# A four-layer graph network: X centred early, the GRU output centred by the matrix that turns it back, the next norm in column groups, and 36 idle products on TensorE

## The chip, the core and the metric

The kernel runs on one core of one Trainium2 chip. The metric is the device time of one execution in microseconds, the median of the runs. A core has five engines with a queue each, which work in the order of their queues and wait for each other by semaphores: TensorE (PE in the profile; its weight loads are PEld), VectorE (DVE), ScalarE (ACT), GpSimd (POOL) and SyncE (SP), which here issues the transfers.

## The reference, cut to what matters

X has 3327 rows of 64 numbers, `adj` is 3327 x 3327. Four layers run one after the other, each as X = X + layer(norm(X)), where the norm takes off each row's mean, divides by the root of its variance and is followed by a ReLU: a hyperbolic layer, a decayed sum over the graph, a signed graph attention whose output goes through two GRU cells, and a second hyperbolic layer. The part that this change touches is the end of the third layer and the start and end of the fourth:

```python
def _layernorm(x, axis=-1, eps=1e-5):
    m = jnp.mean(x, axis=axis, keepdims=True)
    v = jnp.var(x, axis=axis, keepdims=True)
    return (x - m) / jnp.sqrt(v + eps)
...
    def gru_cell(x, h, w_ih, w_hh, b_ih, b_hh):
        ...
        n = jnp.tanh(inn + r * hn)
        return (1.0 - z) * n + z * h
```

The third layer adds to X the sum of the two GRU outputs, each row scaled by that row's diagonal element of `adj`. The fourth layer takes the norm of that X, needs the row's norm squared (`x2` in the kernel) and ends in X plus a combination of the normed row and a sum over the graph.

## The kernel before, in words

Rows are padded to 26 tiles of 128 (T = 26, P = 128, D = 64), so X lies in SBUF as 128 x 26 x 64. The tiles are worked on in two halves of 13 (`HALVES`), and in the third layer tile t of the first half and tile t of the second half are paired, 64 columns each, in turned arrays of 128 x 1664 (`oP`, `hP`, `deg`, `xh`), where a row is a feature and a column is a node. These arrays go through in four column groups (`COLS`: 4, 3, 3 and 3 tiles, 512 or 384 columns).

`hyperbolic_series` (L350) is called twice, for the first and for the fourth layer. In both calls it first prepares: mean, centring, squares, variance, root by bit trick with polish steps (`root_by_bits`), the norm `x2` of the positive part (L449 to L469), then factors, the normed rows `Xr` (L481), their 16-bit parts `hi` (L482, ScalarE) and `lo` (L484, VectorE), and their turning by TensorE (L542, L517) with copies out of PSUM by ScalarE and VectorE (L524, L522). POOL makes further columns (L436 to L506). Weights are multiplied in L560, summed in L562, and spread over the partitions in L576 and its copies. Then the loop over the 4 x 26 tiles of the adjacency runs (ScalarE's sigmoid L629, POOL's mask L632, TensorE's L643 and L644, ScalarE's arctangent L649, VectorE's L654, TensorE's sums L664 and L672). In the fourth layer the factors of each row follow (L736 to L860), and then the end: ScalarE scales `M` tile by tile (L923, 22 of them), VectorE scales and adds (L916, L919), and SP stores X in three pieces (L2104).

`plain_gat` (L1841) is the third layer: 26 blocks of masked sums (L1871) with small pieces of work hung on to them by a table (`todo`, block number to function), then `take`, `mean`, and eight steps of the GRU (two cells x four groups; `products` L1987 and L1992, `sigmoids`, `before_tanh`, `tanh`, `state`). `turn_back` (L2032) turns the sum of the GRU terms of a group back to node rows on TensorE, by products with the identity that accumulate up to four terms (L2043), or by a transpose for the last group (L2041); `scale` multiplies by the diagonal element (L2059 on ScalarE, 64 columns at a time; L2054 on VectorE for the last group); `use` adds to X (L2063). The eight PSUM banks are halves of four tiles: 0 and 1, 2 and 3, 4 and 5, 6 and 7. Group k is turned into bank 4 + k.

The order on ScalarE, VectorE, TensorE and POOL is that in which the program writes the instructions (`manual_schedule`); waits are put in by the tile framework from reads and writes, and a pool that takes over another pool's space waits tile by tile. The order at the end of the third layer is written out:

```python
                tanh(K - 1)
                scale(0)
                turn_back(1)
                scale(1)
                turn_back(2)
                state(K - 1)
                use(0)
                turn_back(3)
                use(1)
                scale(2)
                scale(3)
                use(2)
                use(3)
```

Of the kernel before, what the change touches and what calls it, by code (L numbers as in the profile page):

```python
# [49 lines left out]
def tile_gnn4(ctx: ExitStack, tc: tile.TileContext, x, adjT, att0, b0, w1, bias1, w_gat, a_gat,  # L50
# [296 lines left out]
            after.append(of_r)  # L347
        return wlr, bcol, cc, sqc, isqc, um2, maxn2

    def hyperbolic_series(r, params, ok, masks=None, done=None, ahead=None, then=None, checks=None):  # L350

# [10 lines left out]


        KE = D + 9
        left_row = rows[0 if r is None else 1]
        W = 512
        with ExitStack() as st:
# [60 lines left out]
            with room(name="hsp", bufs=1) as tp, room(name="hsps", bufs=2, space=PSUM) as ps, \  # L430
                    tc.manual_schedule(engines={mybir.EngineType.Activation, mybir.EngineType.DVE,
                                                mybir.EngineType.PE, mybir.EngineType.Pool}):
                H, R, sq, sr = [tp.tile([P, T, D], F32, name=n) for n in ("H", "R", "sq", "sr")]
                Xe = tp.tile([P, T, KE + 9], F16, name="Xe")
                E, Fe = Xe[:, :, D:KE], Xe[:, :, KE:]
                G.memset(X0, 0.0)  # L436
                G.memset(E[:, :, 6:], SX)
                for k, part in enumerate(f16_parts((1.0 - PB / PA) * SX)):
                    G.memset(Fe[:, :, 6 + k:7 + k], part)
# [4 lines left out]
                    return tp.tile([P, T], F32, name=name)  # L444


                mean, v, rv, ax, ia2 = [new(n) for n in ("mean", "v", "rv", "ax", "ia2")]
                for ts in HALVES:
                    V.reduce_sum(mean[:, ts], X[:, ts, :], axis=AX.X)  # L449
                V.tensor_scalar(mean, mean, 1.0 / D, None, op0=OP.mult)  # L450
                for ts in HALVES:
                    V.tensor_sub(H[:, ts, :], X[:, ts, :], wide(mean[:, ts]))
                    A.activation(sq[:, ts, :], H[:, ts, :], AF.Square)
                for ts in HALVES:
                    A.activation(R[:, ts, :], H[:, ts, :], AF.Relu)
                    A.activation(sr[:, ts, :], R[:, ts, :], AF.Square)
                for ts in HALVES:
                    V.reduce_sum(v[:, ts], sq[:, ts, :], axis=AX.X)
                V.tensor_scalar(v, v, 1.0 / D, LN_EPS, op0=OP.mult, op1=OP.add)
                sd, q1, q2 = new("sd"), new("q1"), new("q2")  # L460
                steps = root_by_bits(sd, q1, q2, v)
                next(steps)
                V.reciprocal(rv, v)
                for _ in range(3):
                    next(steps)
                V.reduce_sum(x2[:, HALVES[0]], sr[:, HALVES[0], :], axis=AX.X)
                for _ in steps:
                    pass
                V.reduce_sum(x2[:, HALVES[1]], sr[:, HALVES[1], :], axis=AX.X)  # L469
                if r is not None:  # L470
                    V.tensor_scalar(rv, rv, cc, None, op0=OP.mult)
                V.tensor_mul(x2, x2, rv)
                V.tensor_scalar(ax, x2, 1.0, None, op0=OP.subtract)
                V.reciprocal(ia, ax)
                V.tensor_scalar(root, x2, 1.0, None, op0=OP.max)
# [90 lines left out]
                    copy_on(on, XF[c][:, o, :], turned16(lambda t: Xp[:, t, D:], KE, *range(t, t + c[1])))  # L566
                V.tensor_mul(right, lr[:, :, 1], z)
                V.tensor_scalar(right, right, bcol, None, op0=OP.add)
                V.scalar_tensor_tensor(root, root, ROOT, zs, op0=OP.mult, op1=OP.mult)
                V.tensor_scalar(small["k"], ia, 0.5 * PF, None, op0=OP.mult)  # L570
                V.tensor_scalar(small["bx"], ax, -1.0, None, op0=OP.mult)
# [340 lines left out]
            with room(name="hse", bufs=1) as tp:  # L912
                ah, am = all_factors(tp)

                def scaled(a, f, ts):
                    V.tensor_mul(a[:, ts, :], a[:, ts, :], wide(f[:, ts]))  # L916

                def added(a, ts):
                    V.tensor_add(X[:, ts, :], X[:, ts, :], a[:, ts, :])  # L919

                own = slice(T - 4, T)
                for t in range(own.start):
                    A.activation(M[:, t, :], M[:, t, :], AF.Copy, scale=am[:, t:t + 1])  # L923
                for ts in HALVES:
                    scaled(Xr, ah, ts)
                    added(Xr, ts)
                scaled(M, am, own)
                for ts in HALVES[0], slice(T // 2, T - 6), slice(T - 6, T):
                    added(M, ts)
                    done(ts)  # L930
# [907 lines left out]

            then(H, hparts, banks, last_x, finish, close)

    def plain_gat(masks, zo, deg, first, wg, gru, H, parts, banks, last_x, finish, close):  # L1841

# [6 lines left out]
        with ExitStack() as st:  # L1851
# [47 lines left out]
            xh = [[pers.tile([P, HP], F32, name=f"xh{g}{o}") for o in range(2)] for g in range(2)]  # L1899
            oP = H.rearrange("p k o d -> p (k o d)")  # L1900
            wgT = pers.tile([D, D], F32, name="wgT")
            hundred = pers.tile([P, 1], F32, name="hundred")
            V.memset(hundred, -100.0)
            for _ in range(1):
# [35 lines left out]
                def inverse2():  # L1940
                    V.scalar_tensor_tensor(deg, deg, -1.0, r0, op0=OP.mult, op1=OP.mult)
                    V.scalar_tensor_tensor(deg, deg, 2.0, r0, op0=OP.add, op1=OP.mult)

                todo = {3: lambda: degrees(2, 4), 4: lambda: degrees(3, 6), 12: lambda: (weights2(4), inverse()),
                        13: lambda: turn(0, 6), 15: lambda: weights3(5), 17: inverse2, 19: lambda: turn(4, 7),
                        20: lambda: turn(8, 4), 23: lambda: turn(12, 6)}
                V.tensor_scalar(zo[:, 2 * T:2 * T + 2], zo[:, 2 * T:2 * T + 2], first, None, op0=OP.mult)
# [84 lines left out]
                def turn_back(k):  # L2032

                    terms = [oP] if k == C - 1 else [oP, hP, deg] if k > 1 else [oP, xh[0][0], hP, deg]
                    t0, n = COLS[k]
                    pt = turned[k] = bank(4 + k)
                    for t in range(n):
                        cs = slice((t0 + t) * P, (t0 + t + 1) * P)
                        for i, src in enumerate(terms):
                            if len(terms) == 1:  # L2040
                                PE.transpose(pt[:, t * P:(t + 1) * P], src[:, cs], ident)  # L2041
                            else:
                                PE.matmul(pt[:, t * P:(t + 1) * P], src[:, cs], ident, start=i == 0,  # L2043
                                          stop=i == len(terms) - 1)

                def of_bank(k):
                    n = COLS[k][1]
                    return turned[k][:, :n * P].rearrange("p (t h d) -> p h t d", h=2, d=D)

                def scale(k):  # L2050
                    t0, n = COLS[k]
                    o = scaled[k] = tp.tile([P, 2, 4, D], F32, name="x", bufs=2)
                    if k == C - 1:
                        V.tensor_mul(o[:, :, :n, :], of_bank(k),  # L2054
                                     d2[:, :, t0:t0 + n, None].to_broadcast([P, 2, n, D]))
                        return
                    for h in range(2):
                        for t in range(n):
                            A.activation(o[:, h, t, :], of_bank(k)[:, h, t, :], AF.Copy, scale=d2[:, h, t0 + t:t0 + t + 1])  # L2059

                def use(k):
                    t0, n = COLS[k]
                    V.tensor_add(X2[:, :, t0:t0 + n, :], X2[:, :, t0:t0 + n, :], scaled[k][:, :, :n, :])  # L2063

                for k in (2, 3):
                    mean(k)
# [18 lines left out]
                tanh(K - 1)  # L2085
                scale(0)
                turn_back(1)
                scale(1)
                turn_back(2)
                state(K - 1)  # L2090
                use(0)
                turn_back(3)
                use(1)
                scale(2)
                scale(3)
                use(2)
                use(3)

    def load():
        for ts in HALVES:  # L2100
# [10 lines left out]
    wt, bias, wg, gru = middle_weights()  # L2111
    zo = const.tile([P, 2 * T + 2 + EARLY + len(LATE)], F32, name="zo")
    first = const.tile([P, 1], F32, name="first")
    V.memset(first, 0.0)
    for o in (0, D):
        V.memset(first[o:o + 1, :], 1.0)
    with ExitStack() as ms:
        mid, rs = [ms.enter_context(ExitStack()) for _ in range(2)]
        masks = [None] * (T // 2)
        degs = []  # L2120

        def make_masks(ks):
            pool = ms.enter_context(room(name=f"masks{ks[0]}", bufs=1, side="right"))
            for k in ks:
                masks[k] = pool.tile([P, 2, NP], F8, name=f"mask{k}")

        def right():
            make_masks(range(T // 2 - EARLY // 2))
            pool = rs.enter_context(room(name="middle", bufs=1, side="right"))
            degs.append(pool.tile([P, NP // 2], F32, name="deg"))  # L2130
            return degs[0]

        make_masks(range(T // 2 - EARLY // 2, T // 2))
        pool = mid.enter_context(room(name="own", bufs=1))
        own = [pool.tile([P, 2, CW], F32, name=f"own{k}") for k in range(2)]
        hyperbolic_series(None, params, ok[:, 0:1], ahead=Ahead(masks, zo, own),
                          then=lambda e: plain_decay(
                              e, right, masks, zo, wt, bias, gru, of_r[0],
                              lambda *a: plain_gat(masks, zo, degs[0], first, wg, gru, *a)))
        rs.close()  # L2140
        mid.close()
        hyperbolic_series(r3, params3, ok[:, 2:3], masks, store, checks=Late(zo))
    V.reduce_sum(ok[:, 1:2], zo, axis=AX.X)


# [55 lines left out]
```

## Time and profile before

| what | value |
|---|---|
| median of 3 runs | 721.02 us (720.81 to 722.56) |
| the profiled execution's own time | 719.45 us |
| its span, first to last instruction | 717.7 us |
| mean granted TensorE clock | 0.972 of full |
| busy: TensorE, VectorE, ScalarE, POOL | 636.2, 532.8, 542.1, 433.4 us |

The stretches around the change, from the windows of the profile (busy us; clock as a share of full):

| stretch, us from the start | what runs | PE | DVE | ACT | POOL | clock |
|---|---|---|---|---|---|---|
| 382.9 to 426.9 | blocks of the attention | 43.98 | 14.55 | 19.38 | 0.00 | 0.96 |
| 426.9 to 447.4 | GRU steps | 20.14 | 17.83 | 18.77 | 0.79 | 1.00 |
| 447.4 to 461.3 | turning back, adding to X | 9.14 | 8.47 | 6.09 | 0.55 | 1.00 |
| 461.3 to 474.7 | norm of the fourth layer | 0.00 | 12.79 | 6.06 | 2.50 | 0.56 |
| 474.7 to 485.0 | turning and weights | 9.57 | 9.63 | 6.36 | 5.17 | 0.74 |
| 485.0 to 695.0 | loop over the adjacency | 208.06 | 153.90 | 180.90 | 172.81 | 1.00 |
| 695.0 to 705.3 | factors of each row | 0.16 | 9.25 | 1.10 | 0.00 | 0.67 |
| 705.3 to 717.7 | scaling, adding, storing | 0.00 | 6.07 | 5.36 | 0.00 | 0.50 |

Busy times of a stretch are sums over one engine's instructions; an engine whose busy time is near the stretch's length sets its pace, and where none is near it, they wait for each other. In a timeline row the first two numbers are start and duration, and a bracket gives the idle time ahead of the instruction and what ended it. Instructions of one engine overlap a little, so a duration is longer than the distance to the next one.

### The profile page before, as it was taken

Reading aid. Unit: us, or ns where it says so; the run is one execution under the profiler, and the core shown is the slowest. Engines: PE = TensorE matmul, PEld = TensorE weight load, DVE = VectorE, ACT = ScalarE, POOL = GpSimd, SP = SyncE. Lnnn points to the kernel's source line nnn. Section 1 sums busy time; section 2 is a strip of 40 time slices with the busy share of each in tenths; the row PEclk is TensorE's granted clock in tenths of the full one; section 3 lists DMA queues with packets and bytes.
Section 4 is the critical chain, followed back from the end, with each engine's and each line's share of the span. In section 5 each row is a group of like instructions: output and inputs, shape, how many; then the busy total and the mean of one; then the engine's idle time right before and its main releaser. Section 6 shows DMA issues by size and latency. Waiting matters only on the chain.

```text
span 717.7 us, 12120 instructions
## 1 busy us (share of the span) xinstructions
PE 636.2 (89%) x4291; PEld 261.4 (36%) x4291; DVE 532.8 (74%) x990; ACT 542.1 (76%) x718; POOL 433.4 (60%) x329
## 2 busy tenths in 40 slices
PE   0799999999999889989998999459999999999970
PEld 0522233333333333435445653443223433333320
DVE  5967778777777799999755428697776877778756
ACT  3688888888888695687881479359888888888853
POOL 2799999989999400205730000039888788887840
PEclk9999999999999999999999999969999999999995
DMA  3998888898878716489960000203325345443001
GB/s 64 313 301 274 259 268 266 277 288 273 268 245 271 258 69 215 137 291 333 402 243 1 2 1 1 95 18 96 89 82 147 105 120 146 116 119 115 25 1 52
DMA packets 61638, 119.25 MB, mean 166 GB/s; under 512 B 9568, under 2 KB 34048, under 8 KB 61568
## 3 DMA queue, kind: packets, MB, share of 16 engines
q1 hardware_dynamic: 57216, 118.38, 51.2%
q10 hardware_dynamic: 4352, 0.02, 0.3%
q8 instruction: 35, 0.57, 0.3%
q14 instruction: 35, 0.29, 0.1%
HBM read 115.64 MB, written 0.88 MB: 162 GB/s over the span
## 4 chain that ended last, share of the span: by engine, by line
PE 67%; DVE 12%; issue 6%; POOL 6%; ACT 4%; DMA 3%; ACTq 1%; POOLq 0%; DVEq 0%
PE slot L664 17%; PE slot L672 9%; PE slot L643 9%; PE slot L1564 9%; PE slot L644 8%; POOL sig L632 6%; PE slot L1578 5%; PE slot L1871 5%; DMA adj<-in 3%; PE slot L1987 2%; PE slot L2043 1%; PE slot L1992 1%; DVE X L1617 1%; ACTq L322 1%; ACT sig L629 1%
## 5 line engine op out<-in xcount | busy, mean ns | idle before, releaser
L654 DVE SCALAR_TENSOR_TENSOR sig<-slot,sig 128x768 f32<-128x768 f32 (+2 forms) x209 | 212.8, 1018 | 105.6 <-POOL sig L632 104.2
L649 ACT ACTIVATE slot<-slot 128x768 f32<-128x768 f32 (+1 forms) x208 | 177.2, 852 | 53.3 <-PE slot L644 53.1
L632 POOL TENSOR_TENSOR sig<-adj,sig 128x768 f32<-128x768 f32 (+2 forms) x105 | 201.7, 1943 | 12.9 <-ACT sig L629 8.4
L629 ACT ACTIVATE sig<-leftB,right 128x768 f32<-128x768 f32 (+2 forms) x210 | 203.5, 970 | 0.5 <-PE pt L517 0.5
L632 POOL TENSOR_TENSOR sig<-mask,sig 128x768 f32<-128x768 fp8e4 (+3 forms) x106 | 173.6, 1651 | 38.2 <-ACT sig L629 37.3
L664 PE MATMUL slot<-sig,Xr 128*64 128x384 f32 (+1 forms) x832 | 169.9, 526 | 3.7 <-DVE sig L654 3.4
L643 PE MATMUL slot<-XC,XT 128*128 128x384 f16 (+1 forms) x416 | 142.2, 342 | 3.1 <-ACT sum L682 1.7
L644 PE MATMUL slot<-XF,XE 73*128 73x384 f16 (+1 forms) x416 | 141.6, 340 | 0.0
L672 PE MATMUL slot<-sig,X 128*32 128x384 f32 (+1 forms) x832 | 94.2, 525 | 0.0
L1570 ACT ACTIVATE w<-slot,ebias 128x832 bf16<-128x832 f32 x76 | 69.0, 951 | 25.3 <-PE slot L1564 24.9
L664 PEld LDWEIGHTS slot<-sig,Xr 128*64 128x64 f32 x832 | 49.8, 135 | 85.7 <-issue 62.7
L643 PEld LDWEIGHTS <-XT 128*128 128x128 f16 x416 | 40.6, 98 | 93.8 <-issue 67.4
L1564 PE MATMUL slot<-mask,rest 128*128 128x416 fp8e4 x208 | 53.9, 341 | 5.0 <-ACT adj L1570 2.8
L1564 PE MATMUL slot<-mask,after 128*128 128x416 fp8e4 x208 | 53.4, 339 | 1.3 <-DVE deg L1588 1.3
L644 PEld LDWEIGHTS <-XE 73*128 73x128 f16 x416 | 40.8, 98 | 28.6 <-issue 4.0
L1459 DVE TENSOR_SCALAR_CACHE_REDUCE same<-late 128x832 fp8e4<-128x832 f32 x48 | 48.4, 1009 | 0.0
L219 POOL TENSOR_TENSOR mask<-mask,offdiag 128x128 fp8e4<-128x128 fp8e4 x26 | 17.5, 684 | 44.4 <-PE slot L1564 44.3
L436 POOL MEMSET X<- 128x832 f32 x2 | 1.6, 791 | 69.6 <-ACT xh L1978 69.6
L1871 PE MATMUL slot<-mask,own 128*64 128x384 fp8e4 (+1 forms) x416 | 39.6, 345 | 2.6 <-DVE deg L1588 2.6
L672 PEld LDWEIGHTS slot<-sig,X 128*32 128x32 f32 x832 | 16.4, 108 | 67.7 <-issue 67.7
L542 PE MATMUL pt<-ident_h,Xp 128*64 128x128 f16 x32 | 2.6, 314 | 37.7 <-ACT Xp L482 37.7
L1578 PE MATMUL slot<-w,h 128*64 128x416 bf16 x304 | 34.0, 345 | 0.0
(341 smaller groups left out, 696.2 us busy)
## 6 DMA issues: line engine op xcount, KB each, us to landing
adj<-in SPq DMA_DIRECT2D x78, 384.0 KB, 5.2
late<-in SPq DMA_DIRECT2D x48, 416.0 KB, 3.2
adj<-in SPq DMA_DIRECT2D x17, 832.0 KB, 7.2
adj<-in SPq DMA_DIRECT2D x27, 512.0 KB, 5.8
ahead<-in SPq DMA_DIRECT2D x14, 832.0 KB, 7.7
ahead<-in SPq DMA_DIRECT2D x16, 416.0 KB, 5.7
own<-in SPq DMA_DIRECT2D x16, 416.0 KB, 5.8
own<-in SPq DMA_DIRECT2D x8, 832.0 KB, 10.1
```

Source lines behind the costliest of these rows:

```text
L629: A.activation(sig[:, os], leftB[c][:, os], AF.Sigmoid, bias=right[:, b:b + 1])
L632: G.tensor_tensor(sig[:, os], adj[:, os], sig[:, os], op=OP.mult)
L643: PE.matmul(L[:, o, :c[1] * P], XT[:, rows], XC[c][:, o, :], start=True, stop=False)
L644: PE.matmul(L[:, o, :c[1] * P], XE[:KE, rows], XF[c][:, o, :], start=False, stop=True)
L649: A.activation(L, L, AF.Arctan, scale=PA / SX ** 2)
L654: V.scalar_tensor_tensor(sig[:, os], slot[:, os, :tiles[k][0][1] * P], PC, sig[:, os], op0=OP.add, op1=OP.mult)
L664: PE.matmul(acc[c][o * D:(o + 1) * D, 0, :n], Xr[:, b, :], sigs[k][:, o, :], start=b == 0, stop=b == T - 1)
L672: PE.matmul(acc[c][q:q + 32, 1, :n], X0[:, b - 1 + i, :], w[:, o, :], start=b == 1, stop=b == T - 1, tile_position=(0, q))
L1564: PE.matmul(cnt[o][:, h, :BK], w, cols(k, o, h), start=w is after and steps[k][1] == T - 1, stop=True, skip_group_check=True)
L1570: A.activation(ws[k][:, o, :, :], cnt[o][:, :, :BK], AF.Exp, scale=-LN2, bias=ebias)
L1578: PE.matmul(acc[c][o * D:(o + 1) * D, h, :BK], parts[i][:, b, :], w[:, o, h, :], start=b == T - 1 and i == 0, stop=b == 0 and i == 1)
L1871: PE.matmul(acc[k][o * D:(o + 1) * D, :], w, mask[:, of(k, o * HP)], start=n == 0 and i == 0, stop=n == T - 1 and i == 1)
```

## The change

The mean of X is taken off X early, in block 12 of the attention (`centre`), and kept in `ln.mean`. The GRU output is turned back by products with a matrix `centring` of 130 columns in place of the identity: the identity less 1/64 within each half of 64, which takes off the row mean, and two columns that give that mean. The means of the GRU output, scaled, go to `dm` and are added to `ln.mean`. The groups go to banks 4 and 5, 6, 0 and 2. The norm's squares, variance and `x2` are computed by column groups in tiles that the GRU no longer needs, and the fourth layer takes `H = X`, `rv` and `sd` from there. At the end the mean comes back as the bias of L923, and for the last four tiles by four activations in the preparation. 36 products of `ident_bf` with a slice of `diag` go into bank 7, which nobody reads. `X0` is zeroed by ScalarE in the fourth layer. The first layer's preparation is unchanged (`ln` is None there; it only moves into a branch).

```diff
+                if ln is None:
+                    G.memset(X0, 0.0)
+                else:
+                    A.activation(X0.rearrange("p t e -> p (t e)"), X[:, HALVES[0], :].rearrange("p t d -> p (t d)"),
+                                 AF.Copy, scale=0.0)
...
+                else:
+                    H, rv, sd = X, ln.rv, ln.sd
...
-                V.tensor_mul(x2, x2, rv)
+                V.tensor_mul(x2, x2s, rv)
...
+                if ln is not None:
+                    for t in range(own.start, own.stop):
+                        A.activation(X[:, t, :], X[:, t, :], AF.Identity, bias=ln.mean[:, t:t + 1])
...
-                    A.activation(M[:, t, :], M[:, t, :], AF.Copy, scale=am[:, t:t + 1])
+                    A.activation(M[:, t, :], M[:, t, :], AF.Identity, scale=am[:, t:t + 1], bias=ln.mean[:, t:t + 1])
...
+            BACK = P + 2
+            centring = pers.tile([P, BACK], F32, name="centring")
+            means = centring[:, P:]
+            G.memset(means, 0.0)
+            for o in range(2):
+                G.memset(means[o * D:(o + 1) * D, o:o + 1], 1.0 / D)
+            V.tensor_sub(centring[:, :P].rearrange("p (o d) -> p o d", o=2), ident.rearrange("p (o d) -> p o d", o=2),
+                         wide(means))
...
+                def centre():
+                    V.reduce_sum(ln.mean, X, axis=AX.X)
+                    V.tensor_scalar(ln.mean, ln.mean, 1.0 / D, None, op0=OP.mult)
+                    V.tensor_sub(X, X, wide(ln.mean))
-                todo = {3: lambda: degrees(2, 4), 4: lambda: degrees(3, 6), 12: lambda: (weights2(4), inverse()),
+                todo = {3: lambda: degrees(2, 4), 4: lambda: degrees(3, 6), 12: lambda: (weights2(4), inverse(), centre()),
...
-                    pt = turned[k] = bank(4 + k)
...
+                    for i in range(0, n, 3):
+                        m = min(3, n - i)
+                        pt = bank((4, 6, 0, 2)[k] + i // 3)[:, :m * BACK].rearrange("p (t x) -> p t x", x=BACK)
+                        for t in range(m):
+                            cs = slice((t0 + i + t) * P, (t0 + i + t + 1) * P)
+                            for s, src in enumerate(terms):
+                                PE.matmul(pt[:, t, :], src[:, cs], centring, start=s == 0, stop=s == len(terms) - 1)
+                        turned.setdefault(k, []).append(pt)
...
+                def new_means(k):
+                    t0 = COLS[k][0]
+                    for pt in turned[k]:
+                        ts = slice(t0, t0 + pt.shape[1])
+                        V.tensor_mul(dm[:, :, ts], pt[:, :, P:].rearrange("p t h -> p h t"), d2[:, :, ts])
+                        t0 = ts.stop
...
+                def use_at_once(k):
+                    t0, n = COLS[k]
+                    for h in range(2):
+                        for t in range(n):
+                            to = X2[:, h, t0 + t, :]
+                            V.scalar_tensor_tensor(to, of_bank(k, h, t), d2[:, h, t0 + t:t0 + t + 1], to,
+                                                   op0=OP.mult, op1=OP.add)
+                sq, pos, sr = xh[1][0], xh[1][1], xh[0][1]
...
                 tanh(K - 1)
                 scale(0)
                 turn_back(1)
-                scale(1)
                 turn_back(2)
                 state(K - 1)
+                turn_back(3)
                 use(0)
-                turn_back(3)
-                use(1)
+                squares(0)
+                positive(0)
+                use_at_once(1)
+                new_means(0)
+                new_means(1)
+                squares(1)
+                variance(0)
+                variance(1)
+                for _ in range(36):
+                    PE.matmul(bank(7), ident_bf, diag[:, :4 * P], start=True, stop=True)
                 scale(2)
                 scale(3)
+                use(3)
+                squares(3)
                 use(2)
-                use(3)
+                squares(2)
+                for k in (0, 1, 3, 2):
+                    if k:
+                        positive(k)
+                    squares_of_positive(k)
+                variance(3)
+                variance(2)
+                V.tensor_scalar(ln.v, ln.v, 1.0 / D, LN_EPS, op0=OP.mult, op1=OP.add)
+                steps = root_by_bits(ln.sd, *ln.qs, ln.v)
+                next(steps)
+                V.reciprocal(ln.rv, ln.v)
+                for between in (lambda: new_means(2), lambda: new_means(3),
+                                lambda: V.tensor_add(ln.mean, ln.mean, dm.rearrange("p h t -> p (h t)"))):
+                    next(steps)
+                    between()
+                norms2(0, COLS[2][0])
+                for _ in steps:
+                    pass
+                norms2(COLS[2][0], C2 - COLS[2][0])
```

`squares(k)` is ScalarE's square of the group's X into `sq`, `positive(k)` its ReLU into `pos`, `squares_of_positive(k)` the square of that into `sr`; `variance(k)` and `norms2` are VectorE's row sums of `sq` and `sr`.

## The prediction, made before the changed kernel was run

> **What bounds the kernel now.** I read the page first. Its slices show TensorE busy nearly everywhere, with one hole around slices 26 and 27, where the granted clock also falls:
>
> ```profile
> PE   0799999999999889989998999459999999999970
> PEclk9999999999999999999999999969999999999995
> ```
>
> One slice is 17.9 us, so the hole lies near 460 us, at the seam of the graph attention and the second hyperbolic layer. The timeline there (start, duration, engine, line, tiles, idle before and its releaser) says what the seam is made of:
>
> ```profile
> 450.88 0.39 PE L2043 MATMUL slot<-ident,deg 128*128 128x128 f32 x2
> 451.30 1.74 ACT L2059 ACTIVATE x<-slot,dcol 128x64 f32<-128x64 f32 x8 [0.41 <-PE slot L2043]
> 452.86 0.56 DVE L2027 TENSOR_TENSOR own<-hP,deg 128x384 f32<-128x384 f32 x1
> 453.10 0.49 PE L2043 MATMUL slot<-ident,own 128*128 128x128 f32 x2 [1.83 <-ACT x L2059]
> ...
> 457.89 0.49 PE L2041 MATMUL slot<-ident,own 128*128 128x128 f32 x3
> 458.42 1.33 ACT L2059 ACTIVATE x<-slot,dcol 128x64 f32<-128x64 f32 x6 [1.00 <-PE slot L2041]
> 459.78 0.56 DVE L2054 TENSOR_TENSOR x<-slot,dcol 128x384 f32<-128x384 f32 x1 [1.78 <-ACT x L2059]
> 460.26 1.02 DVE L2063 TENSOR_TENSOR X<-X,x 128x384 f32<-128x384 f32 x2
> 461.31 1.95 DVE L449 TENSOR_REDUCE mean<-X 128x13 f32<-128x832 f32 x2
> 463.50 1.96 DVE L452 TENSOR_TENSOR H<-X,mean 128x832 f32<-128x832 f32 x2
> 464.56 1.83 ACT L453 ACTIVATE sq<-H 128x832 f32<-128x832 f32 x2 [4.81 <-DVE H L452]
> 465.49 1.95 DVE L458 TENSOR_REDUCE v<-sq 128x13 f32<-128x832 f32 x2
> 467.48 0.18 DVE L459 TENSOR_SCALAR v<-v 128x26 f32<-128x26 f32 x1
> 470.17 1.01 DVE L469 TENSOR_REDUCE x<-sr 128x13 f32<-128x832 f32 x1
> 474.74 0.64 PE L542 MATMUL pt<-ident_h,Xp 128*64 128x128 f16 x8 [16.36 <-ACT Xp L482]
> 476.26 2.96 PE L517 MATMUL pt<-ident_h,Xp 128*128 128x128 f16 x26
> ```
>
> Two things are to be seen. The second turning back waits for ScalarE's scaling of the first (1.83 us), because banks 4 and 5 are halves of one PSUM tile. Then everything runs in series on whole halves of X: add, mean, subtract, square, reduce, root. TensorE stands idle 16.4 us. The windows around the hole give the clock (columns: busy us of the five engines, clock, DMA share, GB/s); the last row is the same preparation in the first layer:
>
> ```profile
> 462.00:463.00 1.00, 0.00 (x0) 0.00 (x0) 1.00 (x2) 0.00 (x0) 0.00 (x0) 0.98 1.04 389
> 463.00:464.00 1.00, 0.00 (x0) 0.00 (x0) 0.93 (x3) 0.00 (x0) 0.00 (x0) 0.50 0.77 310
> 480.00:481.00 1.00, 0.84 (x12) 0.66 (x12) 0.91 (x4) 0.47 (x1) 0.00 (x0) 0.99 0.41 83
> 22.00:23.00 1.00, 1.00 (x16) 0.83 (x11) 1.00 (x3) 0.20 (x2) 0.92 (x2) 1.00 0.87 234
> ```
>
> Last, the end, which the change also touches:
>
> ```profile
> 705.36 5.36 ACT L923 ACTIVATE M<-M,am 128x64 f32<-128x64 f32 x22 [5.20 <-DVE am L860]
> 709.34 2.03 DVE L919 TENSOR_TENSOR X<-X,M 128x832 f32<-128x832 f32 x3
> ```
>
> ScalarE ends at 710.72; VectorE's third addition begins at 710.81. They are level: any time added to L923 is added to the end.
>
> **Part 1, work moved early, at nothing.** The mean of X (reduce, scale, subtract over 1664 columns: 1.95 + 0.18 + 1.96 = 4.1 us by L449, L450, L452) goes to block 12, behind L1934, which ends at 401.0. VectorE then waits 9.74 us for ScalarE before L1941. The cover holds; without it the 4.1 us would delay L1941, whose result is first needed at 427. The matrix costs three small memsets on a POOL that is idle from 380 to 438, and one 128x128 subtraction (0.2 us) while TensorE streams blocks until 426.9.
>
> **Part 2, turning back.** Each 128-column fp32 product now takes 130 columns: 0.224 us apart today, so 0.227. The last group becomes products instead of transposes (0.11 to 0.23 each). The turns go to banks 4/5, 6, 0, 2, so the wait of 1.83 us is gone. From 447.4: 40 products, 40 x 0.227 = 9.1, tail 0.2: TensorE ends at 456.7 (now 458.4). The groups end at 451.3, 454.0, 456.1, 456.7. Group 2 also needs state(6), done at 451.3, and group 3 state(7), done at 453.4: neither is late.
>
> **Part 3, norm by groups.** VectorE's queue is now the limit. From rows: addition of 384 columns 0.56 (0.47 apart), of 512 0.69 (0.60 apart), 64-column fused add 0.197 apart (four L1617 took 0.87), independent small op 0.10, dependent 0.21. ScalarE: 384 columns 0.51, 512 0.61.
> - state(7) ends and scale(0) is in at 453.4; use(0) to 454.0; six fused adds of group 1 (1.2) to 455.2; three small products of means to 455.5.
> - squares(0) and (1) lie on ScalarE meanwhile (done 454.8, 455.8); variance(0), (1) on VectorE to 456.6.
> - scale(3) at 456.8, use(3) done 457.9; scale(2), six at 0.2, from 456.1 to 457.45; use(2) done 458.4.
> - squares(3), (2) done 458.5 and 459.0; variance(3), (2) done 459.55.
> - The scalar steps from there: now L459 at 467.48 leads to L469's end at 471.18, 3.7 us. The new list has three more small operations (0.3) and norms over 896 and 768 columns instead of 832 and 832: 3.85. Its inputs, squares of the positive part, end on ScalarE at 460.4 (groups 0, 1) and 462.2 (all): in time. So 459.6 + 3.85 = 463.4.
>
> The mean, the subtraction and L453 to L456 have left the seam. 471.18 - 463.4 = 7.8 us gained.
>
> X0's zeroing moves from POOL to ScalarE (0.9 us), ahead of L482's two copies. By the order of the pools X0 lies over the tile of squares, so it waits for the last norm: 463.4 to 464.4. L482 is not ready before 463.4 + 2.6. Hidden; 0.9 us at most if not.
>
> **Part 4, 36 products.** L643 shows one 512-column 16-bit product each 0.2175 us: 7.8 us. They queue behind the last turn and the reads of bank 6 (same tile): 456.7 to 464.5. What stands behind them is L542, ready at 463.4 + 3.56 = 467.0. No delay, 2.5 us spare. After the last product of today the clock stayed up 4.6 us (458.4 to 463), so 2.5 us of idling should keep it up. At half rate they would take 15.6 us, to 472.3, and hold L542 by 5.3 us.
>
> What is a warm clock worth? The Trainium skill (TensorE: Matmul & The Clock Gate, "What's actually happening") has the clock halved when idle and restored after some 3.4 us of work: by it the 5.3 us from 474.74 to 480 would run in half, and 2.6 us be won. The row says otherwise: in those 5.3 us VectorE goes without a gap from the second L484 through copies and root steps to L562 at 480.27, 0.15 us after it could. TensorE finishing sooner wins that 0.15. Also, L517 takes 2.96 us in the first layer too, under a recorded 1.00: the record doesn't show a cold start. I take 0.15; bounds 0 and 1.
>
> **Part 5, the mean put back.** Four one-bias activations (about 1.05 us) go before ScalarE's leftB copy, which waits 1.83 us for TensorE: hidden. The 22 of L923 get a second per-partition operand. Here a rule speaks against the change: the skill (ScalarE: Activation LUTs, "What ACT_TABLE_LOAD costs") adds about 93 ns for each pointer operand. No row here has two. With one, 64 columns take 0.333 (0.239 apart); without, L1928's 128 columns take 0.270, so 64 about 0.22: the first pointer costs about 0.1. Read as one fetch the second is free; by the rule 22 are 0.332 apart and end at 712.76, not 710.72. VectorE's third addition then begins 1.97 us later, and SP's last store and the branch behind it with it. I take the rule, since the first pointer obeys it; bounds 0 and +2.0.
>
> **Sum.** -7.8 - 0.15 + 1.97 = -6.0. The profiled execution took 719.45 us (span 717.7); I expect a span near 711.8. The median 721.02 stands 0.2% above that execution; the same difference gives 715.1.
>
> **Rivals.**
> - The second pointer is free: -7.95, 713.1. For it: both are [128,1] reads ahead of the same stream. Against: the first is paid for.
> - The seam shrinks less. Every group crosses engines (product, scale, add, square, reduce), and six of these hand-overs could cost 0.3 to 0.6 us more each than my 0.04: 2 to 4 us lost, 717 to 719. For it: DVE waits "issue" of 0.2 to 0.8 us at 708 and 709. Against: the present seam's hand-overs are short.
> - The idle clock is paid for: warm TensorE brings 1 us or more, 714 or below. Against: VectorE's full queue.
> - Slower: the filler products delay the layer. If their release comes only with the last read of a turned bank (the means of group 3, about 460.5), TensorE has idled 3.8 us; at half rate (0.435 each, 15.7 us) they end at 476.2, L542 starts 1.4 us later than today, and with the end's 2.0 us the time is 724.4. From a filler end past 472.9 the change loses. Against: group 3 lies in another tile, so they start warm, straight behind 40 products.
> - The change doesn't do what it says: X's norm moved but the last turn still sets VectorE's pace. It does already in my list, through use(3) and use(2).
>
> **How the numbers follow.** Likeliest, rule and list hold: 0.58, 714.1 to 716.1. Free pointer or paid clock: 0.19, 712.5 to 714. Seam shrinks less: 0.17, of it a third within 0.3% (about 2.2 us, what a measurement here can tell from no change). Slower by filler: 0.04, and 0.02 for anything else. Range 712.6 to 717.9. Faster 0.88, same 0.07, slower 0.05.
>
> **What would show it.** Right: L542 near 467 with idle before it under 3 us; clock 1.00 through 455 to 485; last norm's reduce ending near 463.4; L923's line at 0.33 us apart. Wrong: idle of VectorE at scale(3) or use(2) over 0.5 us; L542 released by the products; a second-layer loop that isn't just shifted.

## The result, and the profile after

The changed kernel takes 714.17 us (median of 4 runs, 713.11 to 714.82) beside 721.37 us for the kernel before in the same runs: ratio 0.9897, 95% interval 0.9879 to 0.9915. The forecast was 715.1. The profiled execution took 714.07 us, span 712.3.

First the page of the kernel after, the same slices as before:

```profile
PE   0799999999999889989998999989999999999960
PEclk9999999999999999999999999999999999999985
```

The hole is gone and so is the 6 in the clock. Then the timeline of the seam:

```profile
456.65 7.93 PE L2172 MATMUL slot<-diag,ident_bf 128*128 128x512 bf16 x35
...
456.85 0.56 DVE L2091 TENSOR_TENSOR x<-slot,dcol 128x384 f32<-128x384 f32 x1 [0.18 <-PE slot L2069]
457.44 1.03 DVE L2101 TENSOR_TENSOR X<-X,x 128x384 f32<-128x384 f32 x2
...
462.64 0.95 DVE L2133 TENSOR_REDUCE wt<-xh 128x12 f32<-128x768 f32 x1
...
467.01 0.41 PE L553 MATMUL pt<-ident_h,Xp 128*64 128x128 f16 x8 [2.43 <-ACT Xp L493]
```

VectorE's wait at scale(3) is 0.18 us, the last norm ends at 463.59, the filler at 464.58 and the layer's first turning product starts at 467.01. But a little later ScalarE meets a wait that the kernel before did not have, ahead of the loop's first sigmoid:

```profile
474.99 0.60 ACT L535 ACTIVATE leftB<-pe 128x512 f32<-128x512 f32 x1 [0.98 <-PE pe L590]
...
477.05 2.38 ACT L643 ACTIVATE sig<-leftB,right 128x512 f32<-128x512 f32 x3 [1.46 <-DVE XE L533]
```

In the kernel before, the sigmoid follows the copy without a wait:

```profile
482.95 0.60 ACT L524 ACTIVATE leftB<-pe 128x512 f32<-128x512 f32 x1 [1.83 <-PE pe L576]
483.45 1.32 ACT L629 ACTIVATE sig<-leftB,right 128x512 f32<-128x512 f32 x2
```

And the end:

```profile
698.80 7.40 ACT L936 ACTIVATE M<-M,mean,am 128x64 f32<-128x64 f32 x22 [5.19 <-DVE am L874]
...
705.57 1.22 DVE L933 TENSOR_TENSOR X<-X,M 128x448 f32<-128x448 f32 x2 [1.29 <-ACT M L936]
```

Single executions differ by up to 3.0 us in when the turning back begins (446.8 to 449.8 us), in a part to which this change adds only what runs hidden in block 12 and before it, and the median of the kernel before moves from 720.4 to 721.4 between the sets of runs below. So I compare traces from that point on: every time in the next table, and below where it says "after the turning back" or gives such a time alone, counts from the first product of `turn_back(0)`. These times repeat to 0.02 us where nothing differs.

| us after the turning back begins | before | after | difference |
|---|---|---|---|
| last norm's reduce ends (L469, L2133) | 23.76 | 15.98 | -7.78 |
| first turning product (L542, L553) | 27.32 | 19.40 | -7.92 |
| sum of weights lr (L562, L573) | 32.85 | 24.71 | -8.14 |
| first sigmoid (L629, L643) | 36.03 | 29.44 | -6.59 |
| scaling of M (L923, L936) begins | 257.94 | 251.19 | -6.75 |
| last addition ends (L919, L933) | 263.95 | 259.18 | -4.77 |
| last instruction | 270.29 | 264.74 | -5.55 |

Up to lr the forecast holds within 0.2 us. Then 1.55 us are lost ahead of the first sigmoid (from lr to it, 4.73 instead of 3.18), 1.98 at the scaling, and 0.8 come back behind the last addition.

### The profile page after: what moved, and what is told of

It is laid out like the page before. It is cut to its first block, busy times and chain, and to the rows that moved or that the text cites. A ratio compares the mean times of both kernels' runs of the same rounds, so it can differ in the third digit from the quotient of the medians.

```text
span 712.3 us, 12219 instructions
## 1 busy us (share of the span) xinstructions
PE 643.0 (90%) x4329; PEld 264.7 (37%) x4330; DVE 534.5 (75%) x1002; ACT 545.5 (77%) x723; POOL 432.1 (61%) x331
## 5 line engine op out<-in xcount | busy, mean ns | idle before, releaser
L643 ACT ACTIVATE sig<-leftB,right 128x768 f32<-128x768 f32 (+2 forms) x210 | 203.5, 970 | 1.7 <-DVE XE L533 1.5
L1622 POOL TENSOR_TENSOR X<-X,bias 128x256 f32<-128x256 f32 (+1 forms) x7 | 5.3, 786 | 44.4 <-DVE Xr L1637 44.4
```

The source lines that it names most:

```text
L643: A.activation(sig[:, os], leftB[c][:, os], AF.Sigmoid, bias=right[:, b:b + 1])
```

## The experiments

**The filler.** Without it, and with twice as much:

```diff
-                for _ in range(36):
-                    PE.matmul(bank(7), ident_bf, diag[:, :4 * P], start=True, stop=True)
```

> The changed kernel without the 36 filler products. Theory (VectorE's full queue sets the pace of the preparation, the clock does not): the same time as the changed kernel, 714.2 within 0.7 us; the turned XC products stand 0.64 us instead of 0.41 us, the layer's first sigmoid moves by 0.3 us at most. Rival (a warm TensorE is worth its halved work): 1 to 2.6 us slower, 715.2 to 716.8.

Median 715.71 us (ratio 0.9935, interval 0.9912 to 0.9958), more than the 0.7 us away that I allowed. lr came at 24.85 instead of 24.71, about the 0.15 of the prediction. The first sigmoid, though, came at 30.58 instead of 29.44, 1.14 us later where I allowed 0.3. The clock was still down when the weights were spread over the partitions (L590). TensorE without filler, then with 36:

```profile
474.89 2.02 PE L590 MATMUL junk<-ident,left 128*128 128x128 f32 x8
```

```profile
472.90 1.16 PE L590 MATMUL junk<-ident,left 128*128 128x128 f32 x8 [0.25 <-DVE left L574]
```

My theory had no place for that. The end came at 265.89 instead of 264.74, a loss of the rival's size; the medians' intervals overlap a little, so this is the word of one trace each.

```diff
-                for _ in range(36):
+                for _ in range(72):
```

> The changed kernel with 72 filler products instead of 36. They should end near 456.7 + 72 x 0.2175 = 472.3 us and hold the preparation's first turning product, now at 467.0, by 5.3 us. Theory (the products stand in TensorE's queue ahead of the layer): 4.5 to 5.5 us slower, near 719.3; a clock held at full speed through the preparation gives back no more than 0.3 us of it. Rival (they can be passed or hidden, or the warm clock pays): under 3 us slower.

720.07 us (0.999, 0.9966 to 1.0014); the filler ends at 24.74 and the first turning product moves from 19.40 to 24.67: 5.27 us, all of it on the path up to there. From that product to lr only 4.07 us passed instead of 5.31, so 1.2 us were given back where I allowed 0.3. The clock held, and VectorE could work ahead meanwhile; the pair of kernels with the banks alone, below, puts the clock's part at 0.14, and that VectorE's lead gave the rest is argued, not shown. The last instruction came 4.2 us later than with 36, a little less than the 4.5 expected.

```diff
-                for _ in range(36):
+                for _ in range(46):
```

> The changed kernel with 46 filler products, which end 19.15 us after the turning back begins; the layer's first turning product comes at 19.40. Theory (36 are too few: the clock falls for one or two windows of 3.4 us right when the preparation begins, and where it is still down the spreading of the weights takes 2.0 us instead of 1.2): no fall of the clock from the blocks to the end of the loop, the first turning product unmoved at 19.4, the sum lr within 0.2 us of the 24.7 of before, the first sigmoid no later than 29.4, and 0 to 1.2 us won against single executions with 36. Rival (VectorE's queue alone sets the pace): nothing moves by over 0.2 us.

715.13 us (0.9899, 0.9876 to 0.9922). The filler ends at 19.13, the first turning product stays at 19.41, lr at 24.71. But the clock did not hold. Two windows of this kernel (columns as in the prediction):

```profile
472.00:473.00 1.00, 0.84 (x22) 0.68 (x19) 0.93 (x4) 0.43 (x2) 0.52 (x4) 1.00 0.26 61
...
474.00:475.00 1.00, 1.00 (x6) 1.00 (x6) 0.67 (x6) 0.20 (x1) 0.00 (x0) 0.50 0.47 112
```

In them TensorE is at work, and the clock falls between them, 25.1 us after the turning back begins, on the spreading of the weights itself, and the first sigmoid came at 30.64, later than with 36. The expectation was wrong in this execution; in two others with 46 products at the same times (all repairs together, below) the clock held.

All falls between the blocks and the loop last 3.41, 6.83, 13.65 or 17.07 us, multiples of 3.413, and where such a window begins differs between executions. With 36 the clock fell 20.7 us after the turning back for one window in the traces of the changed kernel and of the next experiment, and at 21.3 and 21.7 us for two windows in those of the second pointer. What decides it is not shown. That the preparation's products are too small to keep the clock up is one reading. The idle pieces between them are another: TensorE was busy 2.44 and 2.40 of 3.41 us in the two windows ahead of the fall, and in the two traces where the clock held with 46 it was busy at least 2.59 in each window from the filler's end through the spreading.

**The wait for Xe.** By the order of the pools, the loop's first sigmoid tiles lay over H, R, `sq` and `sr` before, which had long been read; these tiles are no longer made, and Xe has moved into their place, which TensorE reads last.

```diff
+                else:
+                    gap = tp.tile([P, 4, T, D], F32, name="gap")
+                    V.memset(gap[:1, 0, 0, :1], 0.0)
```

> The changed kernel with an unused tile of 26.6 KB a partition ahead of Xe in the fourth layer's preparation, so that Xe lies where it lay before the change and the loop's first sigmoid tiles do not lie over it. Theory (the first sigmoid waits 1.5 us for the last transposes of Xe, because its tile takes over Xe's space): that wait is gone, the first sigmoid starts right behind the copy of leftB, and the kernel is 1.0 to 1.6 us faster, 712.6 to 713.2. Rival (the time between preparation and end is lost elsewhere in the loop): no change, 714.2.

The median, 715.45 us (0.993, 0.9902 to 0.9957), lies above the 712.6 to 713.2 expected and doesn't tell this kernel from the changed one. The trace does: the sigmoid follows the copy at once,

```profile
475.97 0.60 ACT L538 ACTIVATE leftB<-pe 128x512 f32<-128x512 f32 x1 [0.99 <-PE pe L593]
476.46 1.32 ACT L646 ACTIVATE sig<-leftB,right 128x512 f32<-128x512 f32 x2
```

at 27.88 instead of 29.44, and the last instruction comes at 263.42 instead of 264.74. The place of a tile was the whole loss ahead of the sigmoid: from lr to it 3.16 us, where 3.18 passed before the change.

**The second pointer.**

```diff
-                    A.activation(M[:, t, :], M[:, t, :], AF.Identity, scale=am[:, t:t + 1], bias=ln.mean[:, t:t + 1])
+                    A.activation(M[:, t, :], M[:, t, :], AF.Copy, scale=am[:, t:t + 1])
```

> The changed kernel whose last scaling of M (22 activations) takes the scale alone, as before the change; the mean of X is left out of the output of 22 tiles. Theory (each second pointer costs 93 ns and the last addition waits for it): the 22 take 5.36 us instead of 7.40, the last addition ends 2.0 us earlier, the kernel is 1.2 to 2.0 us faster, 712.2 to 713.0. Rival (the end is set by SP's stores and branch, whatever ScalarE does): under 0.6 us faster.

713.87 us (0.9909, 0.988 to 0.9938), above the 712.2 to 713.0 expected.

```profile
700.32 5.36 ACT L936 ACTIVATE M<-M,am 128x64 f32<-128x64 f32 x22 [5.20 <-DVE am L874]
...
704.31 2.03 DVE L933 TENSOR_TENSOR X<-X,M 128x832 f32<-128x832 f32 x3
```

From the scaling's start to the last addition's end 6.02 us instead of 7.99, the 1.97 of the prediction. From there to the last instruction 6.07 instead of 5.55, so 1.46 us remain. In this execution the clock was down for two windows at the spreading, and the first sigmoid came at 30.62; that hides the gain in the totals (264.48 against 264.74).

```diff
+            mean_back(range(14))
             region.close()
...
+                mean_back(range(14, own.start))
                 for t in range(own.start):
+                    A.activation(M[:, t, :], M[:, t, :], AF.Copy, scale=am[:, t:t + 1])
```

> The changed kernel, but the mean is put back on X itself by 22 activations with a bias alone, 14 of them after the loop's last copy and 8 after the tanh, where ScalarE idles; L936 takes the scale alone again. Theory (the second pointer is paid on the path, ScalarE's idle stretches of 3.8 and 5.2 us are free): the scaling takes 5.36 us again, the last addition ends 2.0 us earlier against the loop's end, the span 1.2 to 1.5 us earlier. Rival (the new activations delay the tanh or the additions): less than 0.5 us won, or slower.

714.33 us (0.9895, 0.9873 to 0.9917). The 14 stand behind the loop; the other 8 came to stand in ScalarE's idle pieces of the preparation, not behind the tanh. Neither group delays anything: from the first sigmoid to the scaling 221.79 us (221.75 in the changed kernel), from the scaling to the last instruction 12.04 instead of 13.54. So 1.5 us won, with all of X computed; the first sigmoid was at 30.42, again with two low windows.

**The early mean.**

```diff
-                ... 12: lambda: (weights2(4), inverse(), centre()),
+                ... 12: lambda: (weights2(4), inverse()),
...
                 turn_back(3)
+                centre()
```

> The changed kernel with X's mean taken off behind the last state instead of in block 12 (same three VectorE operations, 4.1 us, now in the seam). Theory (VectorE's queue is the limit of the seam and block 12 hid them): the last norm ends 4.0 us later against the turning back, 20.0 instead of 16.0, and the kernel is 3.5 to 4.1 us slower, near 718. Rival (ScalarE or TensorE sets the seam's pace): under 2 us.

719.57 us (0.9967, 0.9949 to 0.9985). The last norm ends at 19.80 instead of 15.98, 3.82 us later:

```profile
467.98 0.94 DVE L2133 TENSOR_REDUCE wt<-xh 128x12 f32<-128x768 f32 x1
```

VectorE's queue is the limit of the seam, and block 12 hides the three operations. The kernel loses more than the 3.5 to 4.1 us expected: its last instruction comes at 270.07, 5.3 us later. Of the rest, 1.25 us lie between lr and the first sigmoid, where the clock was down from 25.7 to 32.5 us.

**The banks alone, in the kernel before.**

```diff
-                    pt = turned[k] = bank(4 + k)
+                    pt = turned[k] = bank((4, 6, 0, 2)[k])
```

> The kernel before, with only the banks of the turning back changed: groups go to banks 4, 6, 0 and 2 instead of 4, 5, 6 and 7; still transposes with the identity and the old order. Theory (the second turn waits 1.83 us for ScalarE because banks 4 and 5 are one tile): that wait is gone, the last turn ends 1.8 us earlier, but the rest of the seam stays in series on whole halves, so the last norm ends 0.9 to 1.8 us earlier (22.0 to 22.9 us after the turning back instead of 23.8): only a small part of the 7.8 us. Rival (the banks carry the gain): 3 us or more.

718.65 us (0.997, 0.9947 to 0.9992). The last norm ends at 20.88 instead of 23.76: 2.88 us, more than I allowed, and just under the rival's 3. The rows of this kernel behind the third group:

```profile
456.14 1.34 ACT L2059 ACTIVATE x<-slot,dcol 128x64 f32<-128x64 f32 x6 [0.67 <-PE slot L2043]
...
456.46 0.56 DVE L2054 TENSOR_TENSOR x<-slot,dcol 128x384 f32<-128x384 f32 x1 [0.41 <-PE slot L2041]
457.51 1.03 DVE L2063 TENSOR_TENSOR X<-X,x 128x384 f32<-128x384 f32 x2 [0.49 <-ACT x L2059]
```

Three waits are gone, not one. The second turn's 1.83 us for ScalarE is one. ScalarE's scaling of the third group now begins 0.04 us behind that group's own products; before, it began 0.36 us behind them, because it waited for the last group's transposes in the other half of the same tile (most of its 1.00 us of idling was for its own products). And VectorE's scaling of the last group (L2054) no longer stands behind ScalarE's of the third, so the addition follows ScalarE at once and not 0.5 us later.

With the mean late, 3.96 of the 7.78 us at the last norm are left, and the banks alone bring 2.88. About 1.1 us remain for the column groups, the additions of group 1 in one operation each and the matrix. That is a difference of single traces, and no run has these alone.

```diff
+                for _ in range(72):
+                    PE.matmul(bank(5), ident_bf, diag[:, :4 * P], start=True, stop=True)
```

> The kernel with only the banks changed, and 72 filler products behind the last turn, which end near 25.0 us after the turning back begins, before the layer's first turning product (near 26). Theory (a held clock helps the spreading of the weights only where it would have been down there; in the kernel before it was just back up by then): against the kernel with the banks alone the sum lr comes 0 to 0.3 us earlier and the first sigmoid 0 to 1.2 us earlier. Rival (a warm TensorE halves the preparation's TensorE time): 2 us or more.

717.87 us (0.9953, 0.9933 to 0.9973). The clock held from the filler into the loop. TensorE's 26 transposes then wait for VectorE between groups (TensorE's timeline):

```profile
473.56 0.84 PE L517 MATMUL pt<-ident_h,Xp 128*128 128x128 f16 x12
474.60 0.61 PE L517 MATMUL pt<-ident_h,Xp 128*128 128x128 f16 x8 [0.20 <-DVE XC L522]
475.47 0.49 PE L517 MATMUL pt<-ident_h,Xp 128*128 128x128 f16 x6 [0.26 <-DVE XT L522]
```

lr at 29.82 against 29.96 with the banks alone, first sigmoid 32.98 against 33.14: the 0.15 of the prediction. In the banks' kernel the spreading was warm without filler too.

**All repairs together.** Unused tile, 46 fillers, mean in ScalarE's idle time:

> The changed kernel with all three repairs: the unused tile ahead of Xe, 46 filler products, and the mean put back in ScalarE's idle time. Theory (three separate losses of 1.2 to 1.5, 0 to 1.2 and 1.2 to 1.5 us): from the turning back to the end 261.9 us against 264.7, or 711.4 us where the changed kernel takes 714.2; ratio to the kernel before 0.984 to 0.987. Rival (they share one wait): under 2 us won.

711.71 us (0.985, 0.9823 to 0.9876), against 714.17 us and 0.9897 for the changed kernel; the intervals just part. First sigmoid 27.88, last addition 255.84, last instruction 261.91 us after the turning back, as expected. And once more, beside the same kernel without any filler:

> The kernel with the unused tile ahead of Xe and the mean put back in ScalarE's idle time, and no filler products at all. Theory (without filler the clock is down from before the preparation and comes back with a window that begins anywhere; if it is still down at the spreading of the weights, those 16 product passes take 2.0 us instead of 1.2 and the first sigmoid waits for them): lr 0.14 us later than with filler, and the first sigmoid at 28.0 us after the turning back where the clock is up in time, at 29.0 to 29.4 where it is not; 0.1 to 1.5 us slower than with 46. Rival (VectorE's queue hides it all): 0.2 us at most in every execution.

> The kernel with all three repairs once more, on the same chip as the one without filler. Theory: first sigmoid at 27.9 us after the turning back where the clock holds and up to 29.4 where a window of low clock falls on the spreading of the weights; end at 261.9 to 263.4; ratio to the kernel before 0.983 to 0.988, and 0.1 to 1.5 us faster than without filler. Rival: the two are the same.

Without filler 712.17 us (0.9877, 0.985 to 0.9904), with it 712.49 us (0.9892, 0.9852 to 0.9932): the medians can't tell them apart. The traces can. TensorE without filler, then with it:

```profile
472.81 2.02 PE L593 MATMUL junk<-ident,left 128*128 128x128 f32 x8
474.62 1.50 PE L593 MATMUL pe<-ident,left 128*128 128x128 f32 x8
```

```profile
475.08 1.16 PE L593 MATMUL junk<-ident,left 128*128 128x128 f32 x8 [0.82 <-DVE left L577]
476.08 1.06 PE L593 MATMUL pe<-ident,left 128*128 128x128 f32 x8
```

lr differs by 0.14 us, the first sigmoid by 1.49 (29.36 against 27.87), the last instruction by 1.43 (263.28 against 261.85). That is one execution of each. The mean granted clock is on record for every execution: with all repairs it is 0.984 or more in seven of eleven, as in both traces where the clock held, and 0.979 to 0.981 in four. One low window is worth 0.0024 of it (3.41 us at half, in some 710), so one or two more were low in those four, though not necessarily on the spreading. How often that happens, with or without filler, and whether the filler pays, stays open.

## Why the prediction was right, and where its sum was off

- **Part 1** held. `centre` ran from 401.3 to 405.3 us, with VectorE still idle 5.6 us behind it; out of its cover it costs 3.82.
- **Part 2**: the times held (groups end within 0.2 us of the list), but "the wait of 1.83 us is gone" was two thirds of what the banks bring (2.88). The other two waits stood in the prediction's own fence, in the brackets of the rows at 458.42 and 459.78. A product of 130 columns stands 0.223 us from the next, as one of 128 did, and not 0.227. The sum did not suffer, because the list was built forward and not as a difference.
- **Part 3** held: the last norm at 15.98, forecast 16.0 (463.4 - 447.4). VectorE's queue was read rightly as the limit; the rival that every hand-over costs 0.3 to 0.6 us more fell.
- **Part 4** failed in three places. "2.5 us of idling should keep it up": in none of the five traces with 36 did it. "The record doesn't show a cold start" was a misreading of the row at 22 us: the clock's records in that trace begin only at 26.05 us, and the 1.00 ahead of them stands for no record. The products there were as slow as under 0.50 (row below the list). And "I take 0.15" is right for the copies (0.14 and 0.14 in two pairs) but left out the spreading of the weights, where nothing of VectorE's hides TensorE. In the kernel before the clock was back at 480.03 us, 0.8 us before that work, and I took this for its nature; it was luck. Where it is down, the first sigmoid comes about 1.0 to 1.5 us later. The estimate from the Trainium skill's rule of an idle window (TensorE: Matmul & The Clock Gate, "What's actually happening") was 2.6 us won; 1.49 is the most that a pair of traces shows. In the changed kernel's trace the clock was low for the transposes and up for the spreading, so this error did not show in its time.
- **Part 5** held to the hundredth for the last addition: 0.332 us apart, 1.97 us. That the end moves with it was wrong by about a quarter (1.46 us in the second pointer's experiment): with the additions further apart the tail behind the last one shrank from 6.34 to 5.55. Of these 0.79 us, 0.45 lie at SP's last store and its read of the flag behind it (0.86 us before, 0.50 after), and 0.3 in the program's last wait, which I have not explained.
- **The step that was missing**: that the loop is "just shifted". I placed X0 against the tiles of the norm, but not what comes to lie in the room of the four tiles that the change does away with. That cost 1.55 us ahead of the first sigmoid, and 1.3 at the end.

The row of the first layer that part 4 misread; the same products took 0.64 us at 474.74 under 0.50, and 0.41 at 467.01 in the changed kernel under 1.00:

```profile
20.75 0.64 PE L542 MATMUL pt<-ident_h,Xp 128*64 128x128 f16 x8 [20.75 <-ACT Xp L482]
```

The sum, measured from the turning back: -8.1 at lr, +1.55 at the sigmoid, -0.2 in the loop, +2.0 at the scaling, -0.8 in the tail: -5.6, where -6.0 was forecast. That it came so near is luck in part: the 1.55 us at the sigmoid were not forecast, nor were the 0.8 in the tail and 0.2 each at lr and in the loop that made up for most of them. The medians' difference is 7.2 us, with an interval of 6.1 to 8.7 by the ratio. That is more than the traces' 5.6. Only one execution of each kernel has a trace, and the one of the kernel before was 1.9 us faster than its median here; where the rest lies is not shown.

## What to carry to other kernels

Write out the queue of the engine that limits a seam, operation by operation with the durations of rows; it gave the end of this one to 0.02 us, and its steps to 0.2. Then ask of every tile that a change removes what will lie in its place, and who reads that last. If an operand costs time on instructions that the end waits for, move its work to a stretch where that engine idles.

## What the runs showed of the hardware that was not expected

The clock changes in windows of 3.413 us: every low stretch between the blocks and the loop is one, two, four or five of them long. In one of three traces with 46 fillers it fell 5.7 us after TensorE had taken up work again, on small 16-bit products with idle pieces between them; which of the two counts as idling is not shown. The recorded 0.5 is real: where TensorE sets the pace, eight passes of fp32 products took 2.02 us instead of 1.16. Where VectorE's copies set it, the low clock cost 0.14 us at the next sum. A product of 130 columns took no longer than one of 128 (0.223 us apart).
